# First images of a spectral network layer: the second skip and the transform along w one cycle later, and two blocks of modes loaded ahead

## Chip, cores and metric

The kernel runs on one core of one Trainium2 chip. The metric is the device time in microseconds (us) of one execution. Data is float32 throughout.

## Reference

The input x has shape 1 x 256 x 256 x 128 (NHWC). Layer 0 is a gated attention over rows with two biases; it gives x1 and is not touched here. Layer 1 takes x1 (group-normed) as one batch of 256 tokens of 256 x 128 points (h and w below), attends over tokens in a spectral form, and ends in two Fourier layers that mix groups of four tokens. Cut to what matters:

```python
def fno_layer(x, wr, wi, bias, sw, sb, out_hw, norm=False, act=False):
    skip = jnp.einsum('bihw,oi->bohw', x, sw) + sb[:, None, None]     # 4 x 4, pointwise
    xf = spectral_conv(x, wr, wi, bias, out_hw)   # rfft2, keep 32 x 16 modes, mix, irfft2
    if norm:
        xf = instance_norm(xf)
    y = xf + skip
    return jax.nn.gelu(y, approximate=False) if act else y
...
attn = instance_norm(attn + tokens, attn_norm_w, attn_norm_b)
attn = attn.reshape(b * (C // TOKEN_CODIM), TOKEN_CODIM, H, W)
h0 = instance_norm(attn, norm2_w, norm2_b)
h1 = fno_layer(h0, mix_wr[0], mix_wi[0], mix_bias[0], mix_sw[0], mix_sb[0], (H, W), norm=True, act=True)
h2 = fno_layer(h1, mix_wr[1], mix_wi[1], mix_bias[1], mix_sw[1], mix_sb[1], (H, W), norm=True)
out = instance_norm(h2, mon_w, mon_b) + attn
```

## The kernel before

**Data.** The 256 tokens are two halves, 0 and 1, of 128, one token per partition. A token's 32768 points are 16 blocks of 2048 (`NB`; half a block is `HB` = 1024). `blocks`, 16 blocks of 8 KB per partition, keeps the current image of one half in SBUF: `hb[b]`. Within a block the points stand as four rows by four "turns" j by 128 columns (`by_turn`). y is the sum that `attn` normalizes; half 0's y stays in `blocks`, half 1's goes to DRAM (`yd`).

**Stages of the second layer, in order.** `y_blocks` makes y; `first_modes(a)` the modes of the first Fourier layer (to `Gd1` in DRAM); `first_images(a)` the image of h1 from them; `second_modes(a)` (for half 1 `LastModes`) the modes of the second layer (`Gd2`); `output` the result. `first_images(0)` runs alone, after `y_blocks(1, ...)` has made 24 of half 1's 32 half blocks. `first_images(1)` is woven with `output_0`: at each of its yields `output_0` may take one step, and each iteration of the one goes with about one block of the other. `first_images(1)` overwrites `hb[b]`, which `output` of half 0 has to have read.

**One block in `first_images`.** TensorE makes the first skip (`ups`, by `skip`, 16 matmuls of 32 x 32 weights and 512 columns, line 1406) and adds the image from the modes (`image`, line 1391), in four PSUM banks of `psk`. ACT applies Gelu from PSUM into `hb[b]` (line 1769). For the block before, TensorE transposes the image by turns (`htps`, line 1781), VectorE copies the transposes to `hT` (lines 1784 and 1793; in half 1 ACT copies one of the four), TensorE makes the second skip (`sps`, line 1406), VectorE takes its `bn_stats` (line 1801), TensorE transforms along w (`psA`, line 1804), ACT copies that to `yA` (line 1806; two buffers) and POOL stores it to `Yd` (line 1807; in half 1 ACT issues the last one). `htps`, `sps` and `psA`, nine tiles per block, go round the four banks of `pst`.

**Sums w (half 0 only).** The last stage needs w = lam * y + x1 of half 0. For half blocks done while half 1's y was made, `Sums` has stored it to `wd`. The others are made in `first_images(0)`: `load_w` loads a half of x1 into `xw` (line 1736; s = 0 in y's `yt` tiles, two buffers; s = 1 in one buffer of `wp`), `add_w` lets ACT scale y (line 1746), POOL add (line 1749) and store (line 1750).

**Order.** The stages from here on are under a manual schedule: each engine and each DMA queue (SP's, POOL's, ACT's) executes in the order of the program. SP issues the loads: in an iteration, the modes of block b+1 (`load_modes`, four loads of 64 KB, line 1415), then the x1 halves of b+1. In half 1 it issues the y halves of b+1 (line 1726) and then the modes, and for `output_0` the w block (line 2113) and its modes. POOL issues the stores of `wd`, `Yd` and the output.

**Buffers.** `first_images(0)` uses the pool `hp0`, opened after `mp0` (of `first_modes(0)` and `Sums`) is closed; both take the same memory. In it lie the modes (`gs2`, two buffers), `hT`, `yA` and `xw`. y's pool `xp` lies elsewhere and stays open; its tag `gs` has three buffers for modes.

Of the kernel before, what the change touches and what calls it, by code (L numbers as in the profile page):

```python
# [10 lines left out]
FP = mybir.dt.float32  # L11
AF = mybir.ActivationFunctionType
ALU = mybir.AluOpType
# [5 lines left out]
P = 128  # L19
# [681 lines left out]
def layer1(tc, I, C, ident, x1d, upool, U, Q2, groups, out):  # L701
# [6 lines left out]
    nc = tc.nc  # L708
    NT, H, W = 256, 256, 128
    L = lambda n: I["L1_conv_" + n]  # L710
    with ExitStack() as ctx:
# [86 lines left out]
        wp = gctx.enter_context(tc.tile_pool(name="wp", bufs=3))  # L798
# [35 lines left out]
        with tc.manual_schedule(engines=COMPUTE):  # L834
# [300 lines left out]
            for k, half in enumerate((high64, low64)):  # L1135
                nc.tensor.matmul(
                    ps[high64, NT + 64 * k : NT + 64 * k + 64], graw1[:, high64], ident[:, half],
                    start=True, stop=True,
# [240 lines left out]
        def by_turn(t):  # L1379

            return t.rearrange("p (n j w) -> p j n w", j=4, w=W)

        def rows_of(ps):
            return ps.rearrange("p (n w) -> p n w", w=W)
# [11 lines left out]
        def skip(ps, src, blk, stop):  # L1396


            parts = src if isinstance(src, list) else [src]
            for k, part in enumerate(parts):  # L1400
                n = slice(k * 4 // len(parts), (k + 1) * 4 // len(parts))
                for j in range(4):
                    for i in range(4):
                        r, o = slice(32 * i, 32 * i + 32), slice(32 * (i ^ j), 32 * (i ^ j) + 32)
                        w = blk[r, r] if len(blk.shape) == 2 else blk[r, j]
                        nc.tensor.matmul(rows_of(ps[j][o, :])[:, n], w, part[r, j], start=(k == 0), stop=stop)  # L1406
# [27 lines left out]
        def run(stage):  # L1434
            for _ in stage:
                pass
# [274 lines left out]
                        )  # L1711
                    nc.vector.tensor_copy(h.turn, ps[:, 260:268])

        def first_images(a, wp, yp, psk, pst, first=None):


            h = halves[a]
            ys, gss = {}, {}

            def load(b):  # L1720
                if a == 1:
                    ys[b] = []
                    for k in (2 * b, 2 * b + 1):
                        pool, tag, bufs = (wp, "wx", 1) if k % 3 == 0 else (yp, "yt", 2)
                        ys[b].append(pool.tile([P, HB], FP, tag=tag, name=f"y2_{k}", bufs=bufs))
                        nc.sync.dma_start(ys[b][-1], ydv[:, a, k * HB : (k + 1) * HB])
                gss[b] = wp.tile([P, 4, P], FP, tag="gs2", name=f"gs2_{a}_{b}")
                load_modes(gss[b], h.Gd1, b)

            def load_w(b):  # L1730
                for s in range(2):
                    if 2 * b + s in h.summed:
                        continue
                    t = (yp, "yt", 2) if s == 0 else (wp, "xw", 1)
                    ys[b, s] = t[0].tile([P, HB], FP, tag=t[1], name=f"xw_{b}_{s}", bufs=t[2])
                    nc.sync.dma_start(ys[b, s], x1v[:, a, b * NB + s * HB : b * NB + (s + 1) * HB])

            def add_w(b):

                todo = [s for s in range(2) if (b, s) in ys]  # L1740
                if not todo:
                    return
                t = yp.tile([P, NB], FP, tag="xt", name=f"w0_{b}", bufs=3)
                for s in todo:
                    px = slice(s * HB, (s + 1) * HB)
                    nc.scalar.activation(t[:, px], hb[b][:, px], AF.Identity, scale=h.col[:, 3:4])
                for s in todo:
                    px = slice(s * HB, (s + 1) * HB)
                    nc.gpsimd.tensor_tensor(t[:, px], t[:, px], ys.pop((b, s)), ALU.add)
                    nc.gpsimd.dma_start(wd[:, b * NB + s * HB : b * NB + (s + 1) * HB], t[:, px])  # L1750

            if first is None:
                load(0)
            else:
                ys[0], gss[0] = first
            if a == 0:
                load_w(0)
                add_w(0)
            for b in range(17):
                if b < 15:  # L1760
                    load(b + 1)
                    if a == 0:
                        load_w(b + 1)
                if b < 16:
                    ps = [psk.tile(f"ups_{a}_{b}_{j}") for j in range(4)]
                    skip(ps, [by_turn(y) for y in ys.pop(b)] if a else by_turn(hb[b]), h.bl0, False)
                    image(ps, gss.pop(b), bs4)
                    for j in range(4):
                        nc.scalar.activation(
                            by_turn(hb[b])[:, j], rows_of(ps[j]), AF.Gelu,  # L1770
                            bias=h.turn[:, 2 * j + 1 : 2 * j + 2], scale=h.turn[:, 2 * j : 2 * j + 1],
                        )
                    if a == 0 and b < 15:
                        add_w(b + 1)
                if b > 0:
                    turned = by_turn(hb[b - 1])
                    hT = {}
                    for j in (1, 2, 3, 0):
                        ps = pst.tile(f"htps_{a}_{b}_{j}")
                        for n in range(4):  # L1780
                            nc.tensor.transpose(ps[:, n * P : (n + 1) * P], turned[:, j, n, :], ident)  # L1781
                        t = hT[j] = wp.tile([P, 512], FP, tag="hT", name=f"hT_{a}_{b}_{j}", bufs=4)
                        if j == 0:
                            (nc.scalar.copy if a else nc.vector.tensor_copy)(t, ps)
                            continue
                        v = t.rearrange("p (n c d x) -> p n c d x", n=4, c=2, d=2)
                        if j == 1:
                            v = v[:, :, :, ::-1].rearrange("p n c d x -> p (n c) d x")
                        elif j == 2:
                            v = t.rearrange("p (n c x) -> p n c x", n=4, c=2)[:, :, ::-1]  # L1790
                        else:
                            v = t.rearrange("p (n c x) -> p n c x", n=4, c=4)[:, :, ::-1]
                        nc.vector.tensor_copy(
                            v, ps.rearrange("p (m c x) -> p m c x", m=v.shape[1], c=v.shape[2])
                        )
                yield 0
                if b > 0:
                    ps = [pst.tile(f"sps_{a}_{b}_{j}") for j in range(4)]
                    skip(ps, turned, blk[1], True)
                    for j in range(4):  # L1800
                        nc.vector.bn_stats(hstat[:, 4 * (b - 1) + j, :], ps[j])
                    psA = pst.tile(f"psA_{a}_{b}")
                    for j in (1, 2, 3, 0):
                        nc.tensor.matmul(psA[32 * j : 32 * j + 32, :], bfwd, hT[j], start=True, stop=True)  # L1804
                    yA = wp.tile([P, 512], FP, tag="yA", name=f"yA_{a}_{b}")
                    nc.scalar.copy(yA, psA)
                    (nc.scalar if a and b == 16 else nc.gpsimd).dma_start(
                        h.Yd[16 * (b - 1) : 16 * b].rearrange("(n j) f t -> (j f) n t", j=4),
                        yA.rearrange("f (n t) -> f n t", n=4),
                    )  # L1810
                yield 1

        def turned_blocks(h):
# [277 lines left out]
        def output(a, b, gs, w, psk):  # L2091

            krs, c0 = (halves[a].col[:, k : k + 1] for k in (14, 9))
            ps = [psk.tile(f"h2ps_{a}_{b}_{j}") for j in range(4)]
            skip(ps, by_turn(hb[b]), by_blocks(halves[a].bl0), False)
            image(ps, gs, bs4)
            for j in range(4):
                nc.scalar.activation(  # L2098
                    by_turn(hb[b])[:, j], rows_of(ps[j]), AF.Identity, bias=c0, scale=krs
                )  # L2100
            yield
            for s in range(2):
                px = slice(b * NB + s * HB, b * NB + (s + 1) * HB)
                nc.vector.tensor_tensor(w[s], w[s], hb[b][:, s * HB : (s + 1) * HB], ALU.add)  # L2104
                nc.gpsimd.dma_start(outv[:, a, px], w[s])  # L2105
# [79 lines left out]
        with tc.manual_schedule(engines=COMPUTE | {ENG.SP}):  # L2185
# [9 lines left out]
            with tc.tile_pool(name="mp0", bufs=1) as wp:  # L2195
                y1 = y_blocks(1, br, 0, U1, Sums(wp))
                weave((2.4 * t for t in first_modes(0, wp, tiles(wp), bq, [(wp, "gt", 1)])), y1)
                halves[0].sums = True
                run(y1)
            with tc.tile_pool(name="hp0", bufs=2) as wp:  # L2200
                run(first_images(0, wp, xp, bq, br))
            with tc.tile_pool(name="mp1", bufs=1) as wp:
                y1 = y_blocks(1, br, U1, 32)
                next(y1)
# [208 lines left out]
```

## Time and profile before

| | |
|---|---|
| median of 3 runs (lowest to highest) | 2632.59 us (2629.96 to 2640.34) |
| the profiled execution: time / span | 2628.83 / 2627.1 us |
| mean granted TensorE clock | 0.953 |
| busy: TensorE / VectorE / ACT / POOL | 92% / 77% / 54% / 56% of the span |
| `first_images(0)` | 1957 to 2096 us of the span |
| `second_modes(0)`, rest of y, `first_modes(1)` | 2096 to 2236 us |
| `first_images(1)` with `output_0` | 2236 to 2434 us |
| `LastModes`, output of half 1 | 2434 to 2627 us |

In what follows, "idle before" is the time that an engine stood before an instruction, with the instruction that released it; "PE" is TensorE's matmuls, "PEld" its weight loads, "DVE" VectorE, "SPq" SP's DMA queue. Fast matmuls overlap, so the time of a group is read from its start to the start of the next, not from the sum of durations. The DMA share is that of 16 DMA engines.

### The profile page before, as it was taken

What the parts mean: (1) busy time and instruction counts of PE and PEld (TensorE: products, weight loads), DVE (VectorE), ACT (ScalarE), POOL (GpSimd) and SP (SyncE); (2) the same over time, 40 slices, a digit from 0 to 9 for tenths busy, and PEclk for the clock granted to TensorE, in tenths of its full rate; (3) what the DMA queues carried; (4) which work ended last, traced back from release to release, by engine and by line L of the source; (5) the groups of instructions that cost most, each with busy time, mean ns of one, the idle gap of its engine ahead of it and who ended that gap; (6) DMA issues with size and microseconds to landing.
All of it is one profiled execution on the core that took longest, in us unless ns stands there. A gap on an engine that the chain in (4) does not pass through costs nothing. (4 is left out here: it accounts for less than half of the span.)

```text
span 2627.1 us, 88799 instructions
## 1 busy us (share of the span) xinstructions
PE 2408.6 (92%) x37598; PEld 1548.5 (59%) x37598; DVE 2025.2 (77%) x2876; ACT 1421.4 (54%) x2732; POOL 1474.6 (56%) x1043
## 2 busy tenths in 40 slices
PE   7799999999999999999998999998979978799754
PEld 6555565665655556565554677786754556455533
DVE  7799999999999999999998457567645645356455
ACT  0377888888888888888886232001016401555232
POOL 1299999999999999999996012002136411111011
PEclk9999999999999999999999999999989987899865
DMA  9755565566656666565663011788877764999699
GB/s 366 218 101 103 102 109 104 104 106 108 106 101 109 105 107 107 102 109 102 108 106 63 14 59 64 260 277 286 299 282 263 239 239 133 314 352 331 195 386 345
DMA packets 1016549, 458.49 MB, mean 175 GB/s; under 512 B 831062, under 2 KB 946729, under 8 KB 1009752
## 3 DMA queue, kind: packets, MB, share of 16 engines
q1 hardware_dynamic: 980120, 364.71, 55.2%
q0 software_dynamic: 22832, 81.54, 8.0%
q10 hardware_dynamic: 13200, 6.56, 0.9%
q8 instruction: 298, 4.88, 0.8%
q14 instruction: 99, 0.81, 0.1%
HBM read 317.36 MB, written 135.27 MB: 172 GB/s over the span
## 5 line engine op out<-in xcount | busy, mean ns | idle before, releaser
L422 POOL TENSOR_TENSOR e<-e,b1T 128x1024 f32<-128x1024 f32 x255 | 604.6, 2371 | 83.5 <-ACT e L404 82.9
L427 POOL TENSOR_TENSOR es<-e 128x512 f32<-128x512 f32 x512 | 647.9, 1288 | 0.1
L449 DVE RECIPROCAL av<-av 128x256 f32<-128x256 f32 x256 | 452.2, 1766 | 9.1
L404 ACT ACTIVATE sc<-sc,b2T 128x512 f32<-128x512 f32 x514 | 340.0, 662 | 123.0 <-PE sc L395 110.9
L404 ACT ACTIVATE e<-sc,b2T 128x512 f32<-128x512 f32 x510 | 322.9, 693 | 0.0
L420 DVE TENSOR_TENSOR e<-sc,b1T 128x1024 f32<-128x1024 f32 x257 | 312.2, 1215 | 6.7 <-ACT sc L404 3.5
L395 PE MATMUL sc<-qkT 32*128 32x256 f32 x4096 | 294.5, 401 | 1.7 <-DVE e L420 1.7
L1524 PE MATMUL yps<-xt,mpT 128*128 128x256 f32 x1024 | 248.3, 393 | 29.7 <-DVE yt L1536 14.2
L437 PE MATMUL av<-e,v 128*32 128x256 f32 x4096 | 268.7, 379 | 1.8 <-DVE gate L450 1.7
L395 PEld LDWEIGHTS sc<-qkT 32*128 32x128 f32 x4096 | 185.7, 184 | 113.6 <-issue 52.7
L1524 PEld LDWEIGHTS yps<-xt,mpT 128*128 128x128 f32 x1024 | 192.8, 194 | 74.7 <-DVE yt L1536 19.4
L437 PEld LDWEIGHTS av<-e,v 128*32 128x32 f32 x4096 | 130.1, 109 | 125.9 <-issue 38.5
L1540 POOL DMA_DIRECT2D yd<-yt x32 | 17.4, 545 | 324.1 <-DVE yt L1536 319.5
L367 ACT ACTIVATE qkT<-qk,qb 128x512 f32<-128x512 f32 x256 | 174.0, 680 | 3.1 <-PE qk L337 3.0
L494 ACT ACTIVATE turned<-turned 128x256 f32<-128x256 f32 x256 | 104.4, 408 | 112.1 <-DVE x1b L462 109.8
L337 PE MATMUL qk<-turned,wT_wk 128*32 128x256 f32 x2048 | 163.8, 392 | 0.8 <-DVE g_ve L35 0.8
L337 PEld LDWEIGHTS u<-adft,x 128*32 128x32 f32 x4096 | 118.4, 110 | 74.9 <-issue 74.7
L442 PE MATMUL av<-es,ones 128*32 128x256 f32 x2048 | 160.7, 379 | 1.6 <-POOL es L427 1.6
L2098 ACT ACTIVATE blocks<-h2ps,col 128x512 f32<-128x512 f32 x128 | 88.9, 779 | 130.5 <-PE h2ps L1391 128.1
L345 DVE STREAM_TRANSPOSE turned<-xk 128x1024 f32<-128x1024 f32 x128 | 158.1, 1235 | 0.4 <-DMA xk<-in_L_conv_kv_x_dram 0.4
L337 PE MATMUL qk<-turned,wn_wq 128*32 128x256 f32 x2048 | 157.9, 380 | 0.0
L2105 POOL DMA_DIRECT2D out_dram<-w x64 | 34.2, 534 | 185.4 <-DVE w L2104 173.1
(574 smaller groups left out, 4264.6 us busy)
## 6 DMA issues: line engine op xcount, KB each, us to landing
xt<-x1d SPq DMA_DIRECT2D x128, 512.0 KB, 6.3
U<-in_x_dram SPq DMA_DIRECT2D x32, 1024.0 KB, 10.3
xk<-in_x_dram SPq DMA_DIRECT2D x512, 64.0 KB, 3.0
xk<-in_L_conv_kv_x_dram SPq DMA_DIRECT2D x512, 64.0 KB, 2.5
x1d<-x1b SPq DMA_DIRECT2D x512, 64.0 KB, 2.2
out_dram<-w POOLq DMA_DIRECT2D x64, 512.0 KB, 7.5
x<-x1d SPq DMA_DIRECT2D x126, 256.0 KB, 3.1
y<-yd SPq DMA_DIRECT2D x62, 512.0 KB, 8.7
```

The source lines that it names most:

```text
L337: nc.tensor.matmul(out[hd], w[:, hd], src, start=start, stop=stop)
L345: nc.vector.transpose(turned[:, a : b + 1 : b - a].rearrange("p k (b c) -> p k b c", c=32), t)
L367: nc.scalar.activation(r["qkT"], ps, AF.Identity, bias=self.qb)
L395: nc.tensor.matmul(sc[h // 2][:, h % 2, c * 256 : (c + 1) * 256], qkT[p, 256 + c * P : 256 + (c + 1) * P], qkT[p, 0:256], start=True, stop ...
L404: nc.scalar.activation(r["e"][1][:, :, c, :] if hp and s < NS - 1 else z, z, AF.Exp, bias=b2T[:, c, s : s + 1])
L420: nc.vector.tensor_tensor(e, sc.rearrange("p h x -> p (h x)"), w, ALU.mult)
L422: nc.gpsimd.tensor_tensor(e, e, w, ALU.mult)
L427: nc.gpsimd.tensor_tensor(es, e[:, :, 0, :], e[:, :, 1, :], ALU.add)
L437: nc.tensor.matmul(ps[hd, 0:256], p["v"][:, 2 * (s % 2) + c, hd], r["e"][h // 2][:, h % 2, c, :], start=(c == 0), stop=(c == 1),)
L442: nc.tensor.matmul(ps[32 * h : 32 * h + 32, 256:512], self.ones, r["es"][h // 2][:, h % 2, :], start=True, stop=True,)
L449: nc.vector.reciprocal(rd, rd)
L1524: nc.tensor.matmul(rows_of(ps[j]), mpT[:, sc, tt], by_turn(xt[:, sc])[:, j], start=(sc == 0), stop=False,)
```

## The change

Three edits.

1. `first_images(0)` gets the modes of its first two blocks in tiles of y's tag `gs` (pool `xp`), loaded before the pool `hp0` is opened.
2. In `first_images` of both halves, the second skip with its `bn_stats` and the transform along w with its copy and store are made for block b-2 in iteration b, instead of for b-1; the loop has 18 iterations instead of 17. Within an iteration the first skip of b comes first (in half 1 after the second skip of b-2), then the second skip of b-2, the image of b, the Gelus of turns 0 and 1, the transform of b-2, the Gelus of turns 2 and 3, the transposes of b-1, and in half 0 the sums of b+1. For the last block the transform comes before the second skip. All of it but the last second skip lies before the first yield.
3. In `output` of half 0, VectorE scales and shifts turns 2 and 3, which ACT did; ACT keeps 0 and 1.

```diff
+        def first_modes_tile(b):
+            t = xp.tile([P, 4, P], FP, tag="gs", name=f"gs2_0_{b}", bufs=3)
+            load_modes(t, halves[0].Gd1, b)
+            return t
+
-        def first_images(a, wp, yp, psk, pst, first=None):
+        def first_images(a, wp, yp, psk, pst, first=None, modes=()):
...
+                if b < len(modes):
+                    gss[b] = modes[b]
+                    return
                 gss[b] = wp.tile([P, 4, P], FP, tag="gs2", name=f"gs2_{a}_{b}")
                 load_modes(gss[b], h.Gd1, b)
...
+            def second_skip(b):
+                ps = [pst.tile(f"sps_{a}_{b}_{j}") for j in range(4)]
+                skip(ps, by_turn(hb[b]), blk[1], True)
+                for j in range(4):
+                    nc.vector.bn_stats(hstat[:, 4 * b + j, :], ps[j])
+
+            def along_w(b):
+                hT = hTs.pop(b)
+                psA = pst.tile(f"psA_{a}_{b}")
+                for j in (1, 2, 3, 0):
+                    nc.tensor.matmul(psA[32 * j : 32 * j + 32, :], bfwd, hT[j], start=True, stop=True)
+                yA = wp.tile([P, 512], FP, tag="yA", name=f"yA_{a}_{b}")
+                nc.scalar.copy(yA, psA)
+                (nc.scalar if a and b == 15 else nc.gpsimd).dma_start(
...
-            for b in range(17):
+            for b in range(18):
                 if b < 15:
                     load(b + 1)
                     if a == 0:
                         load_w(b + 1)
+                if a and 1 < b < 17:
+                    second_skip(b - 2)
                 if b < 16:
...
+                    ps = first_skip(b)
+                if not a and 1 < b < 17:
+                    second_skip(b - 2)
+                if b < 16:
                     image(ps, gss.pop(b), bs4)
...
+                    gelu(b, ps, (0, 1))
+                if b > 1:
+                    along_w(b - 2)
+                if b < 16:
+                    gelu(b, ps, (2, 3))
+                if 0 < b < 17:
+                    turn_back(b - 1)
+                if a == 0 and b < 15:
+                    add_w(b + 1)
                 yield 0
...
+                if b == 17:
+                    second_skip(15)
                 yield 1
...
             for j in range(4):
-                nc.scalar.activation(
-                    by_turn(hb[b])[:, j], rows_of(ps[j]), AF.Identity, bias=c0, scale=krs
-                )
+                if a == 0 and j > 1:
+                    nc.vector.tensor_scalar(by_turn(hb[b])[:, j], rows_of(ps[j]), krs, c0, ALU.mult, ALU.add)
+                else:
+                    nc.scalar.activation(
+                        by_turn(hb[b])[:, j], rows_of(ps[j]), AF.Identity, bias=c0, scale=krs
+                    )
...
+            early = [first_modes_tile(b) for b in range(2)]
             with tc.tile_pool(name="hp0", bufs=2) as wp:
-                run(first_images(0, wp, xp, bq, br))
+                run(first_images(0, wp, xp, bq, br, None, early))
```

`turn_back(b)`, `first_skip(b)` and `gelu(b, ps, js)` hold the transposes with their copies, the first skip and the Gelus, as they were written in the loop.

## Prediction

> **What bounds the kernel now.** I read the page's busy row and 40 slices first (TensorE 92% busy, DMA 0.56 to 0.99 in the second layer), then the stretches around the edited code, the chain of waits there, the waits, and the timelines of POOL and SP. `first_images` runs twice: for half 0 at 1957 to 2096 us, for half 1 (woven with `output` of half 0) at 2236 to 2434 us.
>
> Half 0, one iteration in the chain of waits (start, us, what):
> ```profile
> 1997.39 1.09 PE ups L1406 x32
> 1998.48 1.10 PE ups L1391 x32
> 1999.58 1.90 PE htps L1781 x16
> 2001.48 2.33 PE sps L1406 x32
> 2003.80 1.00 PE psA L1804 x8
> 2004.80 1.09 PE ups L1406 x32
> ```
> An iteration takes 2004.80 - 1997.39 = **7.41 us**. The first skip (`ups L1406`) takes 1.09; the second (`sps`), the same matmuls, takes 2.33, because its four PSUM banks are those of the transposes (`htps`) and VectorE has still to copy them out; `psA` then waits for the first `bn_stats`. Without those waits TensorE's work is 1.09 + 1.10 + 1.90 + 1.09 + 1.00 = **6.18**.
>
> The waits of that stretch (us in total, times, longest), for TensorE, SP and ACT:
> ```profile
> PE ups L1391 <- DMA gs<-Gd: 9.3, 1, 9.3
> ...
> SPq L1415 <- DMA wd<-w: 14.2, 1, 14.2
> ...
> ACT yA L1806 <- DMA Yd<-yA: 12.9, 3, 7.5
> ```
> The first image stands 9.3 us because SP may not load its modes before the last `wd` store of the stage before has landed (their tiles share memory). And at the end ACT's `yA` waits for stores that POOL issues late.
>
> POOL, timeline (start, us, idle before and why):
> ```profile
> 2008.81 2.36 POOL L1749 TENSOR_TENSOR w<-w,xw 128x1024 f32<-128x1024 f32 x1 [2.02 <-DMA xw<-x1d]
> ...
> 2016.52 2.35 POOL L1749 TENSOR_TENSOR w<-w,xw 128x1024 f32<-128x1024 f32 x1 [0.48 <-DMA xw<-x1d]
> ...
> 2095.41 0.75 POOL L1807 DMA_DIRECT2D Yd<-yA  x1 [7.13 <-ACT yA L1806]
> ```
> 21 of the 32 sums w (blocks 2 to 8 and 12 to 15) are made here. The second sum of block k, which I call P(k), ends at 1994.36, 2001.77, 2011.17, 2018.87, 2026.66, 2034.35 for k = 3 to 8 and 2061.04, 2068.48, 2077.89, 2085.90 for k = 12 to 15. Where ACT doesn't pace it, the gap is 9.40, 7.70, 7.79, 7.69: mean **8.1, more than TensorE's 7.41**. It is a loop: `xw` for s = 1 has one buffer, so the next load is issued after P(k), lands 3.6 to 5.2 us later or more, and then POOL adds for 2.37.
>
> Stretches: TensorE, its loads, VectorE, ACT, POOL busy, TensorE clock, DMA share, GB/s:
> ```profile
> 1967.00:1977.00 10.00, 8.90 (x92) 5.54 (x96) 0.00 (x0) 2.78 (x4) 0.00 (x0) 0.50 0.42 126
> 1997.00:2007.00 10.00, 10.00 (x189) 5.03 (x186) 5.56 (x10) 6.14 (x9) 8.71 (x7) 1.00 0.98 344
> ...
> 2300.00:2310.00 10.00, 8.19 (x174) 4.84 (x152) 4.72 (x7) 5.24 (x8) 1.73 (x3) 1.00 1.02 354
> 2380.00:2390.00 10.00, 9.35 (x215) 5.19 (x214) 6.35 (x9) 5.70 (x9) 1.78 (x3) 1.00 0.82 244
> ```
> [...] In two-sum blocks DMA is full too. In half 1 DMA is full (0.99 to 1.03) from 2270 to 2380; only its ends have room.
>
> **What the Trainium skill says.** "TensorE: Matmul & The Clock Gate", What's actually happening: an idle window of some 3.4 us halves the clock. The trace agrees: 0.50 after 9.3 us. "VectorE: DVE Perf Modes", The TRN2 errata: a PSUM-source operation costs 120 cycles plus one per element at 0.96 GHz, 658 ns for 512. The trace has 681 for such a copy; I use 681. "DMA: Bandwidth & Descriptors", Issuing engines are not separate DMA queues: SP's and POOL's transfers share 16 engines. It agrees: `xw`, 3.8 us in the median, took 6.6 at a share of 0.98 (issued by 2002.15, used at 2008.81).
>
> **The change, part by part.**
>
> *Early modes.* The 8 loads of 64 KB for blocks 0 and 1 move ahead of the `hp0` pool, into y's `gs` tiles. SP is idle from 1943.73 to 1965.71, and the slots' last readers (u = 19 and 21) end by 1943.6, so they are in by about 1953. Image 0 then follows its skip at 1958.2, and the clock stays up. The wait for the old memory doesn't vanish: the loads of block 2, the `xw` of block 2 and the first `hT` copy now carry it, to 1965.7. So: Gelu 0 1959.4 to 1962.1 (4 x 0.69), skip 1 to 1962.7, image 1 to 1963.8, transposes of block 0 to 1965.7, their copies right then. Block 2's modes are issued from 1965.7 for 2.5 us, so image 2 is at about 1969, against 1983.6.
>
> *Second skip and transform one iteration later, half 0.* No instruction is added. TensorE's order becomes skip b, second skip b-2, image b, psA b-2, transposes b-1: between a copy out of PSUM and its next user there is always other work. VectorE has 8 x 0.62 = 4.96 per iteration, ACT 5.57 (4 Gelu, two scalings, `yA`), both under 6.18. I take 6.3. But POOL's order is the old one (sums of k, `Yd` of k-2, sums of k+1), and SP's too: modes of k+2 stand behind `xw` of k+1, which waits for P(k). So in two-sum blocks image k+2 comes no sooner than P(k) + 8 (0.5 + 2.6 of issue, then about 5 of landing), and TensorE is paced by the 8 us loop. New wait: `yA` (b-2) now stands between Gelu 1 and 2 of block b on ACT, and behind it the last two Gelus, the sums' scalings, and the next skip. It needs the store of b-4: P(b-2) + 0.85 + 0.76 + 6.9 landing = P + 8.5. Image b, held to P + 8, and two Gelus bring `yA` only at P + 10.5, so I add nothing.
> Block 2's `xw` is issued at 1968.2, lands at 1972.3; its sum ends 1974.8 (before 1983.6); P(3) is then 1982 against 1994.4: **-12**. Five gaps of 8 give P(8) = 2022, still -12. Blocks 9 to 11 have no sums: 3 x (7.41 - 6.3) = **-3**, P(12) = 2046 against 2061. Blocks 12 to 15 again at the loop's pace: -15 at P(15) = 2070.5. The tail is unchanged: `Yd` 13 (to 2072.1), landing 7.1, `yA` 15, `Yd` 15, landing 2.7: the first load of `second_modes` goes at 2083 instead of 2098.3. **Half 0: -15.** The stages up to 2236 start from that load and shift whole. Bounds: -9 (only the wait goes) to -22 (the loop at POOL's own 7.24 a block).
>
> *Half 1.* The same move. A block carries 3.75 MB of 2^20 = 3.93e6 bytes, at 354 GB/s 11.1 us; TensorE now takes 10.5 to 10.9. Inside 2270 to 2380 nothing is to be won. At the ends (30 us at 0.93, 2380 to 2430 at 16.2 MB, which need 46 of the 50 us) I take -3; bounds 0 and -8.
>
> *Output of half 0: turns 2 and 3 scaled by VectorE.* 32 operations leave ACT (32 x 0.70 = 22 us) and join VectorE (32 x 0.681 = 22). Both have room in 198 us (108 and 109 busy). The four scalings of a block run two and two, so its banks and its `w` come some 1.4 us sooner; under full DMA that hides. At the start of the stage, where skip and ACT alternate, I take -1; bounds -3 and +3.
>
> Sum: -15 - 3 - 1 = **-19**. Against the profiled execution's own 2628.8 that is 2609.8; the runs' median is 2632.6, 3.8 above it, so 2613.6, given as 2613. A measurement here can tell about 0.5%, 13 us, from no change.
>
> **Rivals.** *A, the loop eats it:* full DMA makes the gaps longer (9.4 instead of 8) as TensorE pushes, and `yA` in the middle of the Gelus stalls. Then 5 + 3 gaps lose about 0.8 each, the 15 becomes 9, half 1 gives nothing: 2624. For it: 0.98 share. Against: the bytes per block don't grow. *B, half 1 gains as well:* earlier requests close DMA's gaps at both ends (-8), and the sums' loop runs at 7.3: -22 - 8 = -30, 2603. For it: 244 GB/s in 2380 to 2390. *C, slower:* in half 1 VectorE's order now is stats b-2, three `hT` copies, two scalings, two adds of 1.17, and the next stats stand behind the adds; `psA` waits for them, `yA` for psA, Gelu 2 and 3 for yA. My sum of that circle: scaling 1.7, adds 2.35, first stats 0.8, psA 1.0, transposes 1.9, skip 1.05, image 1.1 = 9.9. It decides from 11.1, DMA's time. At 13 it costs 16 x 1.9 = 30, less 15: 2648. Nothing in the profile gives the missing 3 us.
>
> **How the numbers follow.** My case 0.55 (2606 to 2619), A 0.20, B 0.17, C 0.08. Faster by over 0.5% are mine and B: 0.72; A is within: 0.20; C 0.08. Range 2598 to 2627: it takes in B and A, and leaves out C and some of each end.
>
> **What would show it.** Right: no 9.3 us wait on `gs`, clock 1.00 throughout, image 0 at 1958; 6.2 to 6.4 us per iteration in blocks 9 to 11 but about 8 in 3 to 8; first `YT` load near 2083; half 1 still at a DMA share of 1.0 and 191 to 198 us long. Wrong: `YT` at 2090 or later, or an iteration of half 1 over 11.1 with DMA not full.

## Result and profile after

| | before | after |
|---|---|---|
| median (lowest to highest) of 13 runs each, same chip | 2629.96 us (2619.9 to 2641.06) | 2616.76 us (2609.25 to 2625.51) |
| ratio to before, 95% interval | | **0.9946 [0.9931, 0.996]**, about -14 us |
| the profiled execution: span | 2627.1 us | 2607.5 us |

Forecast were 2613 us and a gain of 19 against the profile. The two profiled executions differ by 19.6, the runs by about 14.

To compare executions I cut each into stretches that begin and end with an instruction both kernels have: the first `ups` skip of half 0, the first load of `YT` in `second_modes(0)`, the first matmul into `h2ps` (PSUM of `output` of half 0), the first into `z1acc` (PSUM of `LastModes`), the end of the span.

| us | before | after | difference |
|---|---|---|---|
| start to first skip of half 0 | 1957.1 | 1956.8 | -0.3 |
| half 0: first skip to first `YT` load | 141.2 | 126.6 | **-14.6** |
| first `YT` load to first `h2ps` | 137.7 | 132.8 | -4.9 |
| half 1: first `h2ps` to `z1acc` | 210.4 | 208.9 | -1.5 |
| `z1acc` to the end | 180.7 | 182.4 | +1.7 |

Half 0 gave what was forecast. The third row is code that the change doesn't touch. In all thirteen profiled executions on record it took 132.7 to 138.2 us, so 4.9 us is within its scatter.

The waits in half 0 of the kernel after, 1955 to 2085 us (us in total, times, longest), for TensorE and SP:

```profile
PE sps L1406 <- ACT yA L1807: 3.4, 1, 3.4
PE ups L1391 <- DMA gs<-Gd: 3.0, 3, 1.4
...
SPq L1745 <- POOL w L1758: 28.1, 9, 7.0
...
SPq L1415 <- DMA wd<-w: 11.7, 1, 11.7
```

TensorE's stand of 9.3 us for its first modes has become three of at most 1.4. SP still waits once for the last `wd` store of the stage before (11.7 us), since block 2's modes lie in the old memory; only nobody waits for SP then. What SP waits for most is now line 1745, the x1 load, 28.1 us, for POOL's sum (L1758): the loop of the sums.

Stretches (TensorE, its loads, VectorE, ACT, POOL, TensorE clock, DMA share, GB/s):

```profile
1957.00:1967.00 10.00, 9.15 (x168) 4.79 (x151) 4.32 (x9) 5.58 (x9) 3.72 (x4) 1.00 0.44 172
1967.00:1977.00 10.00, 10.00 (x210) 5.92 (x200) 7.45 (x13) 6.37 (x8) 5.69 (x4) 1.00 0.73 216
1997.00:2007.00 10.00, 8.82 (x152) 5.74 (x155) 5.90 (x10) 5.76 (x8) 7.11 (x7) 1.00 0.92 320
2300.00:2310.00 10.00, 9.40 (x231) 5.74 (x216) 8.10 (x12) 5.40 (x8) 1.83 (x3) 1.00 1.03 373
2380.00:2390.00 10.00, 8.84 (x212) 5.27 (x212) 8.18 (x11) 5.09 (x8) 1.83 (x3) 1.00 1.02 380
```

The second row had the halved clock before; it is 1.00 now. In the third, a stretch of blocks with two sums, TensorE is less busy than before (8.82 against 10.00): it has become quicker than the loop and waits for it. POOL's and TensorE's timelines show the same:

```profile
2004.04 2.33 POOL L1758 TENSOR_TENSOR w<-w,xw 128x1024 f32<-128x1024 f32 x1 [1.99 <-DMA xw<-x1d]
```
```profile
2004.79 1.90 PE L1391 MATMUL ups<-k_bsyn,gs 32*128 32x128 f32 x32 [1.18 <-DMA gs<-Gd]
```

POOL stands 1.99 us for its x1 half, and 0.8 us later the image of the next block stands 1.18 us for its modes, which SP could not issue before: they stand behind that x1 half in its queue. The one chain shows up as two waits on two engines.

The end of half 0 is as it was. ACT's last two copies wait for stores that POOL issued late:

```profile
2072.74 0.58 ACT L1807 COPY yA<-psA 128x512 f32<-128x512 f32 x1 [5.85 <-DMA Yd<-yA]
2079.71 0.58 ACT L1807 COPY yA<-psA 128x512 f32<-128x512 f32 x1 [6.38 <-DMA Yd<-yA]
```

And the end of half 1, in the chain of waits (start, us, what):

```profile
2404.67 1.79 PE psA L1805 x8
...
2407.10 8.28 DMA Yd<-yA
...
2415.46 3.34 DMA YT<-Yd
...
2418.84 6.33 PE f1ps L2030 x128
...
2425.17 9.69 PE z1acc L2058 x44
```

The last store of `Yd`, on which everything after hangs, took 8.28 us to land. In the kernel before the same step of the chain is 4.33 us:

```profile
2432.97 4.33 DMA Yd<-yA
```

### The profile page after: what moved, and what is told of

It is laid out like the page before. It is cut to its first block, busy times and chain, and to the rows that moved or that the text cites. A ratio compares the mean times of both kernels' runs of the same rounds, so it can differ in the third digit from the quotient of the medians.

```text
span 2607.5 us, 88724 instructions
## 1 busy us (share of the span) xinstructions
PE 2393.2 (92%) x37598; PEld 1557.0 (60%) x37598; DVE 2051.0 (79%) x2908; ACT 1399.1 (54%) x2700; POOL 1474.4 (57%) x1043
## 5 line engine op out<-in xcount | busy, mean ns | idle before, releaser
L1524 PE MATMUL yps<-xt,mpT 128*128 128x256 f32 x1024 | 246.7, 391 | 22.3 <-DVE yt L1536 15.1
L437 PEld LDWEIGHTS av<-e,v 128*32 128x32 f32 x4096 | 130.1, 109 | 125.9 <-issue 38.5
L1822 ACT ACTIVATE blocks<-ups,turn 128x512 f32<-128x512 f32 x128 | 92.5, 781 | 89.0 <-PE ups L1391 55.8
```

The lines of the kernel that those rows point to most:

```text
L437: nc.tensor.matmul(ps[hd, 0:256], p["v"][:, 2 * (s % 2) + c, hd], r["e"][h // 2][:, h % 2, c, :], start=(c == 0), stop=(c == 1),)
L1524: nc.tensor.matmul(rows_of(ps[j]), mpT[:, sc, tt], by_turn(xt[:, sc])[:, j], start=(sc == 0), stop=False,)
```

## Experiments

The yardstick is half 0, cut finer. P(k) is the end of the second sum of block k, as in the prediction; the "tail" goes from P(15) to the first `YT` load. One profiled execution each, us:

| kernel | first skip to P(3) | P(3) to P(8) | gap | P(8) to P(12) | P(12) to P(15) | tail | sum |
|---|---|---|---|---|---|---|---|
| before | 37.3 | 40.0 | 8.00 | 26.7 | 24.9 | 12.4 | 141.2 |
| after | 23.8 | 42.3 | 8.46 | 23.8 | 23.8 | 12.9 | 126.6 |
| all_again | 25.0 | 42.5 | 8.49 | 24.5 | 24.7 | 12.3 | 129.0 |
| e1_modes | 24.8 | 42.2 | 8.45 | 24.7 | 24.5 | 13.2 | 129.4 |
| e2_order | 36.2 | 41.0 | 8.20 | 24.5 | 24.8 | 12.1 | 138.6 |
| e3_scale | 36.9 | 41.0 | 8.19 | 25.8 | 24.3 | 12.3 | 140.3 |
| e4_half0 | 26.4 | 42.0 | 8.40 | 26.2 | 24.4 | 13.2 | 132.2 |
| e5_xw2 | 23.6 | 36.4 | 7.28 | 23.4 | 21.8 | 12.6 | 117.8 |
| e7_ya4 | 23.6 | 42.5 | 8.51 | 24.9 | 24.8 | 10.6 | 126.3 |
| e8_actyd | 26.7 | 38.9 | 7.77 | 28.6 | 21.6 | 10.1 | 125.9 |
| e9_oldxw2 | 24.8 | 37.1 | 7.41 | 29.6 | 22.3 | 12.1 | 125.8 |

After, all_again and e4_half0 have the same code in half 0 and lie from 126.6 to 132.2: a difference of less than some 5 us in their sum, or 2 to 3 us in one column, shows nothing by itself.

**The three edits, each alone, and all of them** (one chip, medians in us: before 2633.76).

e1_modes, the first edit alone:

```diff
+            early = [first_modes_tile(b) for b in range(2)]
             with tc.tile_pool(name="hp0", bufs=2) as wp:
-                run(first_images(0, wp, xp, bq, br))
+                run(first_images(0, wp, xp, bq, br, None, early))
```

> Edit 1 alone: the modes of half 0's first two blocks are loaded ahead; order and scaling as before. Theory L (half 0 is paced by the loop of the sums, about 8 us per block against TensorE's 7.4 or 6.6, so what counts is when that loop starts): the first sum starts near 1971 to 1973 us instead of 1981, and the first YT load comes at 2084 to 2087, nearly all of the 14.8 us that the whole change gained up to there. In total -12 to -14 us. Rival R (the reordering is what shortens half 0; the modes give only the 9.3 us wait): first YT load near 2089 to 2092, and in total -9 or less.

e2_order, the second edit alone (both halves):

```diff
-            for b in range(17):
+            for b in range(18):
...
+                if not a and 1 < b < 17:
+                    second_skip(b - 2)
...
+                if b > 1:
+                    along_w(b - 2)
```

> Edit 2 alone: second skip and transform one iteration later in both halves; no modes ahead, ACT scales all four turns. Theory L: half 0 gains only 3 to 4 us by its first YT load (2094 to 2096), since the loop of the sums starts as late as before; half 1 (first h2ps to the last Yd store, 197.0 us before, 190.9 in the changed kernel) gains about 4; in total -3 to -8. Rival R: first YT load at 2088 or earlier, in total -12 or more.

e3_scale, the third edit alone:

```diff
+                if a == 0 and j > 1:
+                    nc.vector.tensor_scalar(by_turn(hb[b])[:, j], rows_of(ps[j]), krs, c0, ALU.mult, ALU.add)
```

> Edit 3 alone: VectorE scales two of the four turns of half 0's output. Theory L: half 0 as before (first YT load 2098); half 1 about 2 us shorter (195), total within 3 us of before. Rival S (half 1's 6 us come from the split, because the banks and w come free sooner at its start): half 1 at 191 to 192 by itself, and the order alone gives half 1 nothing.

all_again, the whole change once more:

> The whole change once more, for the same chip as its parts. Both theories: 0.9931 to 0.996 of before, first YT load within 1.5 us of 2083.5. If the parts are independent, the sum of the three alone lies within 4 us of it; under L order and modes overlap in half 0 (both only let the same loop start or run ahead), so the sum of the parts is no smaller than the whole.

| kernel | median | ratio to before [95%] | half 0 | first `h2ps` to `z1acc` |
|---|---|---|---|---|
| e1_modes | 2622.08 | 0.9961 [0.9943, 0.9979] | 129.4 | 212.6 |
| e2_order | 2633.94 | 1.0002 [0.9981, 1.0024] | 138.6 | 215.5 |
| e3_scale | 2633.01 | 0.9998 [0.9982, 1.0015] | 140.3 | 209.8 |
| all_again | 2620.42 | 0.9954 [0.9938, 0.9971] | 129.0 | 212.9 |

By the ratios the early modes alone give about 10 of the whole change's 12 us, and in half 0 all of it (129.4 against 129.0). The new order by itself, the bulk of the diff, gives nothing that can be measured, where 3 to 8 us were expected in total and 4 in half 1; nor do the scalings on VectorE. The table by P(k) says why: e1_modes and the whole change are the same in every column, within a microsecond. The loop of the sums starts 12 us sooner and then runs at its own 8.4 us, whichever order TensorE has. The expectations counted the first `YT` load from the start of the span, and in these four the first skip itself came between 1951.9 and 1969.7 us. Counted from the first skip, e1_modes and e2_order are where theory L had half 0, and all_again is a microsecond above.

**Half 1 in the old order.** e4_half0 has edits 1 and 2 for half 0 only, and ACT does all scalings:

```diff
-                for done in first_images(1, hp, xp, bq, br, ([y2[:, 0:HB], y2[:, HB:]], g2)):
+                for done in first_images_old(1, hp, xp, bq, br, ([y2[:, 0:HB], y2[:, HB:]], g2)):
```

(`first_images_old` is the function of the kernel before.)

> Edits 1 and 2 in half 0 alone: half 1 runs in the old order and ACT scales all four turns. Measured so far, from half 0's first skip to the first YT load: before 141.2 us, whole change 126.7 and 129.0. Theory L (the whole gain lies in half 0; what half 1's new order wins before its last Yd store it pays in that store's landing and behind it, because DMA is full): first skip to YT 126 to 130, first h2ps of half 0's output to the first z1acc matmul 209 to 213 (before 210.4, whole change 208.9 and 212.9), total within 3 us of the whole change. Rival H (half 1's edits are worth the 4 to 6 us by which its stage is shorter): total 4 us or more above the whole change.

Measured: 2622.18 us against 2633.71, ratio 0.9949 [0.9931, 0.9968], the whole change's value; half 1 took 213.2. Half 0, with 132.2, fell outside what was expected, at the upper end of its scatter. With all profiled executions, half 1 from the first `h2ps` to `z1acc`: new order with split scalings 208.9, 213.0, 213.4, 213.4, 209.7, 212.6 and 209.8 (after, all_again, e5_xw2, e5_again, e6_nosums, e7_ya4, e8_actyd), mean 211.55; old order without the split 210.4, 212.6, 213.2 and 209.5 (before, e1_modes, e4_half0, e9_oldxw2), mean 211.43. **In half 1 the change gives nothing that can be measured.**

The chains of waits of all thirteen executions say where it went. From the first `h2ps` to the issue of the last `Yd` store the eight kernels with the new order in half 1 took 190.9 to 197.8 us, mean 194.5; the five with the old order 195.6 to 198.3, mean 196.9. That is 2.4 us gained. But this store took 7.4 to 10.1 us to land in the eight, mean 8.3, and 4.2 to 5.5 in the five, mean 4.9: 3.4 us lost. In the eight, SP begins the group of `YT` loads that precedes this store 1.7 to 4.2 us ahead of it, in the five 5.3 to 7.6 us; that loads so close to it slow the store is possible and was not tested.

**What paces half 0.** Three kernels, each the whole change and one thing more. In e5_xw2 the x1 halves with s = 1 get a second buffer; to make room, all of half 0's modes go through y's three `gs` tiles:

```diff
+                if a == 0:
+                    gss[b] = first_modes_tile(b)
+                    return
                 gss[b] = wp.tile([P, 4, P], FP, tag="gs2", name=f"gs2_{a}_{b}")
...
-                    t = (yp, "yt", 2) if s == 0 else (wp, "xw", 1)
+                    t = (yp, "yt", 2) if s == 0 else (wp, "xw", 2)
```

> The whole change, and half 0's modes all in y's gs tiles (three buffers); the 4 KB this frees give xw for s = 1 a second buffer. Theory L (one xw buffer makes the loop of the sums: load, land, add, 8.5 us per block in the changed kernel): gaps between the second sums of blocks 3 to 8 fall to 7.3 to 7.7, first skip to YT 120 to 124. Rival D (full DMA sets the pace, whatever the buffers): gaps stay at 8 or more and YT stays at 126 to 129.

e6_nosums leaves out the x1 loads and POOL's additions:

```diff
-                    nc.sync.dma_start(ys[b, s], x1v[:, a, b * NB + s * HB : b * NB + (s + 1) * HB])
+                    ys[b, s] = None
...
-                    nc.gpsimd.tensor_tensor(t[:, px], t[:, px], ys.pop((b, s)), ALU.add)
+                    ys.pop((b, s))
```

> The whole change without half 0's x1 loads and additions in this stage: for 21 half blocks wd then holds the scaled y alone, ACT's scaling and the stores stay. Theory L: with the loop gone, TensorE sets the pace, 6.6 to 6.7 us per iteration throughout, no wait of yA on its store, first skip to YT 113 to 118. Rival T (TensorE's own chain with ACT and VectorE is what costs 8 us in the blocks with sums): iterations stay near 8 there and YT at 123 or more.

e7_ya4 has e5_xw2's modes, one `xw` buffer, and four `yA` in half 0:

```diff
-                yA = wp.tile([P, 512], FP, tag="yA", name=f"yA_{a}_{b}")
+                yA = wp.tile([P, 512], FP, tag="yA", name=f"yA_{a}_{b}", bufs=2 if a else 4)
```

> The whole change, and half 0's modes all in y's gs tiles as in the kernel with two xw buffers, but the 4 KB go to yA: four buffers in half 0. Theory L: the gaps of the sums stay at 8 to 8.5, since the loop is untouched, but at the end yA of blocks 14 and 15 needn't wait for landings (5.9 and 6.4 us in the changed kernel); the three last stores leave POOL one after another, first skip to YT 121 to 125. Rival E (the end is set by TensorE's last blocks or by DMA): YT within 1.5 us of the whole change.

| kernel | median (before 2633.71) | ratio to before [95%] | half 0 |
|---|---|---|---|
| e5_xw2 | 2605.37 | **0.9890 [0.987, 0.9911]** | 117.8 |
| e6_nosums | 2600.86 (one run) | | 114.1 |
| e7_ya4 | 2617.66 | 0.9928 [0.9904, 0.9951] | 126.3 |

The second buffer takes 9 to 11 us out of half 0, more than was expected, and the gap falls from 8.46 to 7.28 in blocks 3 to 8 and from 7.94 to 7.27 in blocks 12 to 15. POOL's timeline in e5_xw2:

```profile
2042.87 2.37 POOL L1761 TENSOR_TENSOR w<-w,xw 128x1024 f32<-128x1024 f32 x1
2045.53 0.56 POOL L1762 DMA_DIRECT2D wd<-w  x1 [0.30 <-POOL w L1761]
2046.11 2.39 POOL L1761 TENSOR_TENSOR w<-w,xw 128x1024 f32<-128x1024 f32 x1
2048.80 0.57 POOL L1762 DMA_DIRECT2D wd<-w  x1 [0.30 <-POOL w L1761]
2049.37 0.76 POOL L1811 DMA_DIRECT2D Yd<-yA  x1
2050.15 2.37 POOL L1761 TENSOR_TENSOR w<-w,xw 128x1024 f32<-128x1024 f32 x1
```

No wait on `xw` is left. From one block's first sum to the next, 2050.15 - 2042.87 = 7.28 us, POOL stands only the 0.30, twice, from its own sum to the issue of the store: its queue is full. TensorE in the same kernel has no stand at all in these blocks. Without the sums (e6_nosums) half 0 takes 114.1 us, so the sums still cost e5_xw2 under 4 us. In that kernel TensorE goes from image to image in 1995.11 - 1988.46 = 6.65 us:

```profile
1988.46 1.17 PE L1391 MATMUL ups<-k_bsyn,gs 32*128 32x128 f32 x32
...
1995.11 1.17 PE L1391 MATMUL ups<-k_bsyn,gs 32*128 32x128 f32 x32
```

More `yA` buffers don't take the second buffer's place, and neither do the modes in three `gs` tiles: in e7_ya4, which has these too, the gaps are the loop's (8.51), only the tail is 2 us shorter, and half 0 missed the expectation by a microsecond.

**With the loop out of the way: the order, and POOL's queue** (one chip, before 2632.36). e9_oldxw2 is e1_modes with e5_xw2's buffers, that is, the old order in both halves:

```diff
-                    t = (yp, "yt", 2) if s == 0 else (wp, "xw", 1)
+                    t = (yp, "yt", 2) if s == 0 else (wp, "xw", 2)
```

> Early modes with half 0's modes all in three gs tiles and the second xw buffer, but the old order of second skip and transform, and ACT scaling alone. TensorE takes 7.41 us per iteration in the old order, POOL 7.28 in a block of two sums. If the loop of the sums was all that held half 0, the new order is worth only 0.13 x 10 in the blocks with two sums, 0.75 x 3 in blocks 9 to 11 and some 1 to 3 us at the start: from the first skip to the first load of YT 121 to 124 us against 117.8 of e5_xw2, ratio 0.990 to 0.993. If the order is worth what it was predicted (6.3 against 7.41 in every block), 16 us more than e5_xw2: 132 to 134 us, ratio about 0.995.

e8_actyd is e5_xw2 with half 0's `Yd` stores issued by ACT:

```diff
-                (nc.scalar if a and b == 15 else nc.gpsimd).dma_start(
+                (nc.scalar if not a or b == 15 else nc.gpsimd).dma_start(
```

> The whole change with the second xw buffer and three modes tiles, and half 0's Yd stores issued by ACT (0.37 us each) and not by POOL (0.77). With the second buffer POOL had not a gap in a block of two sums: two adds of 2.37, two wd issues and one Yd issue make 7.28, while TensorE needs 6.66. Theory Q (POOL's queue is the wall there): the block falls to about 6.7, from the first skip to the first load of YT 112 to 114 us against 117.8, span 3 to 5 us below e5_xw2's. Theory D (DMA is the wall as well: a block of two sums moves 1 MB of xw, 0.25 of modes, 1 of wd and 0.25 of Yd, 2.62e6 bytes, which at the 356 to 368 GB/s of e5_xw2's stretches are 7.1 to 7.4 us): the block stays at 7.1 to 7.4, and only the tail gains, since the last three Yd stores no longer stand behind POOL's adds: 114 to 117 us, 1 to 3 us below e5_xw2.

e5_again is e5_xw2 once more:

> The same program as e5_xw2, as the yardstick of this job: ratio 0.987 to 0.991 again, 7.28 us from one second sum to the next, 117 to 119 us from the first skip to the first load of YT.

| kernel | median | ratio to before [95%] | half 0 |
|---|---|---|---|
| e5_again | 2604.28 | **0.9891 [0.9857, 0.9925]** | 117.6 |
| e9_oldxw2 | 2626.4 | 0.9964 [0.9942, 0.9986] | 125.8 |
| e8_actyd | 2622.93 | 0.9958 [0.994, 0.9977] | 125.9 |

e9_oldxw2 settles what the new order is worth. TensorE's timeline there, one iteration from second skip to second skip:

```profile
2005.05 2.40 PE L1406 MATMUL sps<-blocks,blk 32*32 32x512 f32 x32
2007.38 1.06 PE L1816 MATMUL psA<-hT,k_bfwd 128*32 128x512 f32 x8
2008.38 1.16 PE L1406 MATMUL ups<-blocks,bl 32*32 32x512 f32 x32
...
2012.46 2.40 PE L1406 MATMUL sps<-blocks,blk 32*32 32x512 f32 x32
```

7.41 us, and P(k) comes every 7.41: here TensorE's order is the wall. Half 0 is 8 us longer than in e5_xw2, between what the two theories said: 6 of the 8 lie in blocks 9 to 11, where 29.6 us is four iterations of 7.41. The medians differ by 22 us; the first skip came 8 us later in e9_oldxw2's profiled execution than in e5_again's, before anything in which the two differ, and the rest I can't place. The ratio, 0.9964, lies above both theories', though its interval takes in the second's 0.995. All with early modes, half 0 in us:

| | one `xw` buffer | two |
|---|---|---|
| old order | 129.4 | 125.8 |
| new order | 126.6, 129.0, 132.2 | 117.8, 117.6 |

Neither the order nor the second buffer is worth much alone (about 0 and 4, both within the scatter); together they are worth 12. The runs agree: the ratios are 0.9961 for neither, 0.9964 for the buffer, 0.9946 to 0.9954 for the order, 0.989 for both. From neither to both that is 0.7%, 19 us, more than half 0's 12; where the other 7 lie is not shown.

e8_actyd went against both theories: 8 us slower in half 0 than e5_again. The largest part, 5 us, lies from P(8) to P(12). ACT's timeline in blocks 9 to 11, of e8_actyd and then of e5_again:

```profile
2033.79 1.45 ACT L1825 ACTIVATE blocks<-ups,turn 128x512 f32<-128x512 f32 x2 [3.32 <-PE ups L1391]
2035.13 0.58 ACT L1810 COPY yA<-psA 128x512 f32<-128x512 f32 x1
2035.74 0.37 ACTq L1811 DMA_DIRECT2D Yd<-yA  x1
2036.15 1.45 ACT L1825 ACTIVATE blocks<-ups,turn 128x512 f32<-128x512 f32 x2 [0.44 <-ACT yA L1810]
2040.92 1.45 ACT L1825 ACTIVATE blocks<-ups,turn 128x512 f32<-128x512 f32 x2 [3.32 <-PE ups L1391]
```
```profile
2031.69 1.45 ACT L1825 ACTIVATE blocks<-ups,turn 128x512 f32<-128x512 f32 x2 [3.32 <-PE ups L1391]
2033.03 0.58 ACT L1810 COPY yA<-psA 128x512 f32<-128x512 f32 x1
2033.49 1.47 ACT L1825 ACTIVATE blocks<-ups,turn 128x512 f32<-128x512 f32 x2
2038.28 1.45 ACT L1825 ACTIVATE blocks<-ups,turn 128x512 f32<-128x512 f32 x2 [3.32 <-PE ups L1391]
```

An iteration takes 2040.92 - 2033.79 = 7.13 us, in e5_again 2038.28 - 2031.69 = 6.59. The store may be issued only when the copy has ended, and Gelu 2, which in e5_again begins while the copy is still running, stands behind that: it begins 2.36 us after Gelu 0 instead of 1.80. TensorE's next skip waits for those Gelus. The waits of e5_xw2, and then of e8_actyd, over the same stretch:

```profile
PEld ups L1406 <- ACT blocks L1825: 8.0, 19, 1.0
```
```profile
PEld ups L1406 <- ACT blocks L1825: 18.8, 32, 2.8
```

ACT itself stands 3.32 us in each of these iterations, in both kernels: it isn't full, it lies on a circle with TensorE, and the circle grew by what was put into it. So neither POOL's queue nor DMA was tested: another bound came first. From P(12) to P(15) e8_actyd is no slower than e5_xw2 (21.6 against 21.8); the 3 us that it loses before P(3) and the 2 us from P(3) to P(8) I can't place, nor that the medians differ by 19 us. The gain in the tail came as expected (10.1 against 12.4). Issuing only the last stores of half 0 by ACT, where no Gelu is behind them, was not run.

The best version is e5_xw2: 0.989 in two measurements, another 0.6% below the kernel after.

## Why the prediction was right, and where not

**Right by its steps: the early modes.** The image of block 0 follows its skip, the clock stays at 1.00, and image 2 comes at 1969.12 (forecast 1969). P(3) was forecast for 1982 and came at 1980.6; P(8) 2022 and 2022.9; P(12) 2046 and 2046.7; P(15) 2070.5 and 2070.5; the first `YT` load 2083 and 2083.45. That P(8) fits so well is in part luck: P(3) came 1.4 us early, and longer gaps took it back. That the old wait would not vanish but be carried by block 2, where it costs little, held: it is the 11.7 us on SP above. e1_modes shows that this edit alone makes the gain.

**Right: the loop of the sums paces half 0.** It was read from POOL's timeline of the kernel before, where the gaps (8.1) exceeded TensorE's 7.41. e1_modes and all_again agree in every column, and the second buffer moves the gap where nothing else did. Rival A was half right: the gaps grew from 8.00 to 8.46 (five of them: 2.3 us), but not through `yA` in the middle of the Gelus. That wait was forecast at nothing, and both `yA` waits after are in the tail. e1_modes has 8.45 in the old order, so the longer gap comes with the early start and not with the order.

**Right sum, wrong cause: -3 in blocks 9 to 11.** The step was "3 x (7.41 - 6.3)", the new order's gain where there are no sums. P(8) to P(12) did fall by 2.9. But e1_modes, in the old order, has 24.7 there too, and e4_half0, with the new order's code, 26.2: the hit was luck. With one buffer P(8) runs behind TensorE, and P(12) is not four iterations after it; that difference is no measure of TensorE's iteration. The iteration did get shorter, to 6.6 and not 6.3, and with one buffer that was worth nothing. What was counted too low is the second skip, at 1.09 us like the first; in the kernel after the two together last 1975.78 - 1973.12 = 2.66 us, up to the image, instead of 2.18:

```profile
1973.12 1.21 PE L1406 MATMUL ups<-blocks,bl 32*32 32x512 f32 x28
...
1974.19 1.65 PE L1406 MATMUL sps<-blocks,blk 32*32 32x512 f32 x31
1975.78 1.17 PE L1391 MATMUL ups<-k_bsyn,gs 32*128 32x128 f32 x32
```

Why the second isn't shorter stays open.

**Wrong: half 1, -3.** The step "at the ends I take -3" counted on the room in DMA at both ends of the stage. The mean of seven executions against four is +0.1. Up to the issue of its last store the stage did get shorter, by 2.4 us in the mean, close to the forecast. What failed is a term that was put at nothing without a word: the landing of that store, on which the next stage waits. It took 3.4 us longer in the mean, and with the new order in half 1 it always took longer than with the old one (7.4 us at the least against 5.5 at the most). Inside, DMA is full as before (1.03, 373 GB/s). Rival B, a gain in half 1, and rival C, VectorE's circle that would make it slower, are both out.

**Wrong in size, without effect: the scalings on VectorE.** They were priced at 681 ns, by a copy from PSUM. The group in the kernel after:

```profile
L2140 DVE TENSOR_SCALAR blocks<-h2ps,col x32: 798/806/810, 2218.8 to 2392.7; 128x512 f32<-128x512 f32 x32
```

806 ns, which makes 32 x 0.125 = 4 us more VectorE time. None of it shows in e3_scale (0.9998, interval 0.9982 to 1.0015), which can't tell the forecast -1 from 0 either.

**The pair of profiles flattered the sum.** It was to be -19, and the two profiles differ by 19.6. But 4.9 of that lie between the first `YT` load and the first `h2ps`, where nothing changed; e3_scale, with half 0 as before, has 134.6 there, and e1_modes and all_again have 134.4. The kernel before just had a slow execution of that stretch, and the kernel after a quick one; its profiled execution is also the fastest of its 13 runs. The runs say 12 to 14 us, which is half 0's gain alone (-9 to -15 in the profiled executions), and nothing that can be seen for the 4 us of half 1 and the scalings.

## What to carry to other kernels

When a shorter iteration and an earlier start go into the same stage, look first for a loop that runs beside the engine you improve: where one buffer's load, landing and use took longer than the iteration, as here, only the start counted, and the reordering paid once that buffer was doubled. Before you move an instruction to an engine "with room", look at what stands behind it in that engine's queue: a DMA issue of 0.37 us cost 0.5 us per iteration, because it waited for a copy that the next instruction had overlapped with. When a stage ends in a transfer that the next one waits for, price its landing too: here it ate what the stage had gained. Price an edit by several executions of the same stretch; one pair of profiles showed 5 us in code that the change doesn't touch.

## What the runs showed of the hardware

- A VectorE `tensor_scalar` with two per-partition operands, PSUM to SBUF, 512 elements, took 806 ns, where a copy took 681 and `bn_stats` 680. The Trainium skill, "VectorE: DVE Perf Modes", The TRN2 errata, states 120 cycles plus the elements at 0.96 GHz for any operation from PSUM, as an estimate 658 ns for 512; it doesn't tell the two apart, so the measured 806 decides. Whether the operands or something else in the instruction cost the difference was not tested.
- A store of 256 KB at the end of half 1 landed in 7.4 to 10.1 us in the eight kernels with the new order and in 4.2 to 5.5 in the five with the old one, with DMA shares from issue to landing of 0.7 to 0.8 and 0.5 to 0.8: a landing time from another kernel is a rough price, and the share of DMA does not tell it.
- The start of `first_images(0)` came between 1951.9 and 1973.2 us in kernels whose program before it differs in eight loads at the most. The same program gave 1957.8 and 1965.0 (e5_xw2, e5_again): part of the scatter comes from the stages before the edited ones.
